# Summing the states of a scan on TensorE: identity matmul, or transposing matmuls with a copy and a turn back

## The chip, the cores and the metric

One core of a Trainium2 chip runs the whole program. The metric is the device time of one execution in microseconds (us). One execution was also recorded by the hardware profiler; stretches of it are given in us from the start of its span.

## The reference, cut to what matters

The network has an attention layer, six transformer layers, and a state-space layer with an adaptive norm around it. The change sits in the state-space layer. With 16 batch rows of 256 tokens, 256 inner channels d and 16 states n, it computes

```python
deltaA = jnp.exp(jnp.einsum('bld,dn->bldn', delta, A))
deltaB_u = (delta * h)[..., None] * Bm[:, :, None, :]

def step(state, t):
    dA_t, dBu_t, c_t = t
    state = dA_t * state + dBu_t
    y_t = jnp.einsum('bdn,bn->bd', state, c_t)
    return (state, y_t)
...
y = ys.transpose(1, 0, 2) + h * D_param
y = y * _silu(res)
return y @ out_proj_w
```

The einsum in `y_t` is the sum over the 16 states that the title speaks of.

## The kernel before, in words

Activations are kept with features on the partitions and tokens along the free dimension. The state-space stage (class `StateSpace`, run after the transformer) works on eight groups of two batch rows, so a tile is 128 channels by 512 tokens in f32. The 256 channels are two halves, k = 0 and 1, and one scan handles one state n of one half: 32 scans a group, numbered i = 2n + k.

For each i there are these steps: `DA` (ScalarE: the exponential, the decay), `DB` (the input, written to PSUM; for half of the first fourteen states and for the last two it is one VectorE product, kind "D", for the other seven it is four matmuls on TensorE, kind "E"), `SC` (VectorE: the scan itself), `HC` (GpSimd: the state times C) and `Y` (TensorE: adds `HC`'s tile to a sum in PSUM, by a matmul with the identity as the stationary operand; `start` on the first state, `stop` on the last). The two sums `y0` and `y1` have a PSUM bank each, `du` has two, and the other four banks are one pool, `bank()`, which serves `DB`, the transposes and every projection.

After the sums come `YK` (VectorE: y + D u, for each half), `GY` (GpSimd: times the gate), `PY` (TensorE: the output projection) and `XT` (VectorE: the residual). Then a second norm, one more matrix (`MY`, `ME`) and the output.

Before the scans of a group stand its own norm and projections: `L1` (four transposes), `ST`/`AG` (statistics), `RS` (GpSimd: the power -1/2), `NB`, `XN` (ScalarE: normalise, four instructions), `L2` (four transposes back), `HT`, the convolution `PX`, `U`, `PD`, `XD`, `PZ`, then `EE`, `WW`, `LL`, `W2`, `ZF` (the softplus and what follows from it), `DU`, `TD` (transposes for the "E" states), their copies `DT`, and `CDU` (ScalarE: a copy to PSUM for the "D" states). `DG` (ScalarE) scales the identity by B for the "E" states.

No scheduler decides the order: inside `manual_schedule` the instructions of each engine stand in the order in which the steps are called, and `SSM_ORDER` writes that order out. `YK0@2` means: in pass p, do `YK` of half 0 for group p - 2. So one pass mixes the ends of group p - 2, the scans of group p - 1 and the start of group p. A pass opens with `L1` of the new group, the last two `HC` and the last four `Y` of the old one, and `YK`; `DA05`, `DT0`, `DT1` and `DB05` of the next scans follow. In the profile, `Y` is L1434, `YK` L1440, `HC` L1428, `SC` L1424, `DB` L1415 and L1418, `DA` L1409, `DT` L1380, `CDU` L1384, `XN` L1226, `PY` L1450, `XT` L1458; `L1`, `L2` and `M3` share L1204.

Of the kernel before, what the change touches and what calls it, by code (L numbers as in the profile page):

```python
# [10 lines left out]
F32 = mybir.dt.float32  # L11
# [6 lines left out]
P = 128  # L18
B, S, D = 16, 256, 128
NT = S // P  # L20
NTOK = B * S
G = 2
NG = B // G
GT = G * S
# [15 lines left out]
DI, NS, DTR, KC = 256, 16, 64, 4  # L40
# [513 lines left out]
class Transformer:  # L554
# [330 lines left out]
    def Y(self, g, b, i):  # L885
        if i == 0:
            g.py[b] = self.one.take([P, S], "py")
        for h in range(4 * i, 4 * i + 4):
            self.c.nc.tensor.matmul(  # L889
                g.py[b],  # L890
                g.l.wvo[:, h, :],
                self.at[:, h, :],
                start=(h == 0),
                stop=(h == HEADS - 1),
            )
# [136 lines left out]
    def group(self, n):  # L1032
        g = Ctx()
        g.layer, g.b0 = n // NG, n % NG * G
        g.l = self.layers[g.layer]
        g.q = {(k, b, t): Ctx() for k in range(2) for b in range(G) for t in range(NT)}
        for name in ("ss", "r", "qT", "x2", "s", "mx", "pp", "sm", "pT", "pa", "py", "fp"):
            setattr(g, name, {})
        return g
# [47 lines left out]


SSM_ORDER = """
L1@0 HC30@2 ST@0 AG@0 HC31@2 Y28@2 Y29@2 Y30@2 RS@0 YK0@2 Y31@2 YK1@2 DA05@1 GY0@2 BT00@1 NB@0 DT0@1  # L1090
DT1@1 DA03@1 DB05@1 GY1@2 DA01@1 BT03@1 CDU@1 DA00@1 MY@3 DB01@1 XN@0 SC05@1 ME@3 L2@0 SC01@1 PY@2
DA04@1 HC01@1 DB02@1 SC02@1 DB04@1 MA@3 HC02@1 XT@2 SC04@1 HT@0 DB00@1 DA06@1 PX0@0 HC05@1 DA07@1
DG06@1 DA09@1 DA08@1 M3@3 SC00@1 DB07@1 SC07@1 Y01@1 HC00@1 U0@0 Y00@1 DB03@1 MO@3 DB08@1 SC03@1
# [17 lines left out]
class StateSpace:  # L1111
# [318 lines left out]
    def Y(self, g, i):  # L1430
        n, k = divmod(i, NC2)
        if n == 0:
            g.y[k] = self.dp.tile([P, GT], F32, tag=f"y{k}", name=f"y{k}")
        self.c.nc.tensor.matmul(g.y[k], self.c.ident, g.hc[i], start=(n == 0), stop=(n == NS - 1))  # L1434

# [63 lines left out]
    def group(self, i):  # L1501
        g = Ctx()
        g.i, g.b0 = i, i * G
        g.x = self.c.xT[:, i * GT : (i + 1) * GT]
        g.u = g.rs = g.z = g.e = None
        for name in ("px", "pr", "pz", "td", "dT", "bt", "cn", "dg", "da", "db", "s", "hc", "y", "yk"):
            setattr(g, name, {})
        return g

# [269 lines left out]
```

## Time and profile before

| | |
|---|---|
| time, median of 3 runs | 3700.16 us (3696.62 to 3700.87) |
| time of the profiled execution | 3697.34 us, its span 3695.6 us |
| busy over the span | PE 97%, DVE 90%, ACT 77%, POOL 71% |
| first and last scan of the state-space stage | about 3187 to 3672 us |
| `Y`, L1434 | 512 matmul records (two for each of 256 steps), 244.8 us busy |
| `SC`, L1424 | 256 scans, 301.1 us busy, 1208 ns each |

PE is TensorE, PEld its weight loads, DVE is VectorE, ACT is ScalarE, POOL is GpSimd. A wait row names the waiting engine and line, who ended the wait, and the total in us, the number and the longest. A timeline row has the start, the length, the engine, the line, and output <- inputs; a bracket at its end is the idle time just before it and what ended that.

### The profile page before, as it was taken

The page shows a single profiled execution, that of the slowest core. Times are in us where ns is not written, and L with a number is a line of the kernel's source. Part 1 is how long each engine was busy: PE and PEld are TensorE (multiplying, and loading weights), DVE is VectorE, ACT ScalarE, POOL GpSimd, SP SyncE. Part 2 cuts the span into 40 slices and gives each one's busy share as a digit, 9 for nine tenths or more (in the row PEclk, how much of TensorE's full clock was granted, in tenths as well). Part 3 has the DMA queues.
Part 4 walks back from the last instruction along what each step waited for, and adds up shares of the span by engine and source line. Part 5 has one row for each costly group of instructions (what it writes and reads, how often), then busy time and mean ns, then how long its engine had stood idle before and what let it go on. Part 6 is the DMA issues. An engine that isn't in the chain of part 4 may idle for free.

```text
span 3695.6 us, 104087 instructions
## 1 busy us (share of the span) xinstructions
PE 3581.4 (97%) x44976; PEld 2183.2 (59%) x44976; DVE 3343.1 (90%) x4735; ACT 2830.4 (77%) x4056; POOL 2616.4 (71%) x1668
## 2 busy tenths in 40 slices
PE   9999599999999999999999999999999999899997
PEld 5555366666666666666666666666666566555554
DVE  5675599999999999999999999999999998699997
ACT  3676477877877878778778777787788787889895
POOL 2231577777787777877877877777778886588887
PEclk7999699999999999999999999999999999999999
DMA  1100001000010000100001000000000000344442
GB/s 29 38 8 2 1 7 37 5 7 6 6 37 6 6 7 4 37 6 6 7 6 36 7 6 6 13 28 7 6 6 16 12 6 15 99 110 113 112 113 74
DMA packets 85672, 97.15 MB, mean 26 GB/s; under 512 B 9417, under 2 KB 56669, under 8 KB 84445
## 3 DMA queue, kind: packets, MB, share of 16 engines
q1 hardware_dynamic: 85212, 90.49, 9.0%
q8 instruction: 353, 5.78, 0.7%
q14 instruction: 107, 0.87, 0.1%
HBM read 75.26 MB, written 3.94 MB: 21 GB/s over the span
## 4 chain that ended last, share of the span: by engine, by line
PE 75%; ACT 5%; DVE 4%; issue 3%; POOL 1%; DVEq 0%; POOLq 0%; ACTq 0%
PE banks L889 18%; PE banks L679 16%; PE banks L868 10%; PE banks L965 7%; PE banks L810 6%; PE banks L753 4%; PE y L1434 4%; PE banks L1010 3%; ACT kT L770 2%; PE db L1418 2%; DVE s L1424 2%; PE px L1275 1%; ACT qT L770 1%; PE banks L780 1%; POOL u L741 1%
## 5 line engine op out<-in xcount | busy, mean ns | idle before, releaser
L726 POOL TENSOR_TENSOR u<-u,w 128x1024 f32<-128x1024 f32 x384 | 901.8, 2365 | 232.1 <-DVE w L707 149.0
L741 POOL TENSOR_TENSOR u<-u,r 128x1024 f32<-128x1024 f32 x384 | 720.5, 1903 | 129.5 <-DVE r L737 129.5
L679 PE MATMUL banks<-wqk,F 128*128 128x512 f32 x1536 | 727.3, 607 | 3.4 <-DVE w L707 3.4
L889 PE MATMUL banks<-at,wvo 128*128 128x256 f32 x3072 | 711.7, 382 | 0.1
L889 PEld LDWEIGHTS banks<-at,wvo 128*128 128x128 f32 x3072 | 571.7, 190 | 121.5 <-issue 44.6
L689 ACT ACTIVATE sq<-banks 128x512 f32<-128x512 f32 x768 | 425.9, 595 | 239.7 <-DVE u L695 226.1
L707 DVE TENSOR_TENSOR w<-banks,sinl 128x512 f32<-128x512 f32 x768 | 498.4, 673 | 33.0 <-PE banks L679 23.5
L695 DVE TENSOR_TENSOR u<-banks,cosl 128x1024 f32<-128x1024 f32 x384 | 463.7, 1208 | 10.6 <-PE banks L679 9.2
L679 PEld LDWEIGHTS banks<-wqk,F 128*128 128x128 f32 x1536 | 274.9, 191 | 314.4 <-issue 270.0
L719 DVE TENSOR_REDUCE ss<-sq 128x16 f32<-128x1024 f32 x384 | 454.3, 1194 | 3.5 <-ACT sq L689 0.6
L879 ACT COPY at<-banks 128x1024 f32<-128x1024 f32 x384 | 365.8, 1021 | 105.8 <-PE banks L868 105.7
L849 POOL TENSOR_TENSOR pp<-pp,sm 128x1024 f32<-128x1024 f32 x192 | 366.0, 1914 | 62.6 <-ACT sq L689 27.9
L868 PE MATMUL banks<-pT,xw 32*128 32x512 f32 x3072 | 388.6, 613 | 5.2 <-DVE w L707 2.4
L810 PEld LDWEIGHTS banks<-kT,qT 64*32 64x32 f32 x24576 | 262.5, 105 | 151.5 <-ACT sq L689 72.2
L1424 DVE TENSOR_TENSOR_SCAN s<-da,db 128x512 f32<-128x512 f32 x256 | 301.1, 1208 | 18.8 <-PE db L1418 5.6
L810 PE MATMUL banks<-kT,qT 64*32 64x64 f32 x24576 | 295.6, 225 | 3.9 <-issue 3.8
L770 ACT COPY qT<-banks 128x1024 f32<-128x1024 f32 x192 | 194.1, 1014 | 120.3 <-PE banks L753 120.3
L965 PE MATMUL banks<-hT,w 128*128 128x512 f32 (+1 forms) x576 | 265.8, 598 | 4.7
L823 DVE TENSOR_REDUCE mx<-banks 128x16 f32<-128x1024 f32 x192 | 233.1, 1214 | 37.4 <-PE banks L810 29.5
L1434 PE MATMUL y<-hc,ident 128*128 128x512 f32 x512 | 244.8, 604 | 18.9 <-POOL hc L1428 17.2
L868 PEld LDWEIGHTS banks<-pT,xw 32*128 32x128 f32 x3072 | 164.2, 186 | 155.0 <-issue 122.3
L753 PE MATMUL banks<-ident,u 64*128 64x64 f32 x6144 | 228.5, 227 | 24.1 <-POOL u L741 24.1
(235 smaller groups left out, 6210.6 us busy)
## 6 DMA issues: line engine op xcount, KB each, us to landing
btd<-bc SPq DMA_DIRECT2D x72, 512.0 KB
bte<-bc SPq DMA_DIRECT2D x56, 256.0 KB
xw<-xw SPq DMA_DIRECT2D x96, 96.0 KB
wqk<-in_Wqk SPq DMA_DIRECT2D x6, 1024.0 KB
wv<-in_LWvT SPq DMA_DIRECT2D x6, 512.0 KB
wo<-in_Wo SPq DMA_DIRECT2D x6, 512.0 KB
xin<-in_x SPq DMA_DIRECT2D x8, 256.0 KB
out<-ot SPq DMA_DIRECT2D x8, 256.0 KB
```

The source lines that it names most:

```text
L679: nc.tensor.matmul(q.p[:, x], self.F[:, g.b0 + b, o : o + P], g.l.wqk[:, k, x, :], start=True, stop=True)
L689: self.c.nc.scalar.activation(q.sq[:, x], q.p[:, x], AF.Square)
L695: self.c.nc.vector.tensor_tensor(q.u.rearrange("p h x d -> p x h d"), q.p, g.l.cosl[:, t, k].unsqueeze(2).to_broadcast([P, 2, HEADS, DH // ...
L707: self.c.nc.vector.tensor_tensor(q.w[:, :, x], q.p[:, 1 - x], g.l.sinl[:, t, k, x, :].unsqueeze(1).to_broadcast([P, HEADS, DH // 2]), ALU. ...
L719: self.c.nc.vector.tensor_reduce(g.ss[b][:, t, k, :], q.sq.rearrange("p x h d -> p h x d"), AX.XY, ALU.add)
L726: self.c.nc.gpsimd.tensor_tensor(q.u, q.u, q.w, ALU.add)
L741: self.c.nc.gpsimd.tensor_tensor(uf, uf, g.r[b][:, t, k, :].unsqueeze(2).to_broadcast([P, HEADS, DH]), ALU.mult)
L810: nc.tensor.matmul(s[qs, e, j, :], qT[es, j, qs], kT[es, j, ks : ks + 2 * W], start=False, stop=True, skip_group_check=True,)
L868: self.c.nc.tensor.matmul(g.pa[b, t, w // 2][:, w % 2, :], self.xw[b][qs, t, k, :], g.pT[b, t][qs, k, :], start=(k == 0), stop=(k == 1),)
L889: self.c.nc.tensor.matmul(g.py[b], g.l.wvo[:, h, :], self.at[:, h, :], start=(h == 0), stop=(h == HEADS - 1),)
L965: self.c.nc.tensor.matmul(p[0:n, x, :], g.l.w1[:, w : w + n], g.hT, start=True, stop=True)
L1434: self.c.nc.tensor.matmul(g.y[k], self.c.ident, g.hc[i], start=(n == 0), stop=(n == NS - 1))
```

## The change

`Y` no longer multiplies by the identity from the left with 512 columns at once. It takes the `HC` tile in four blocks of 128 columns, each the stationary operand of a transposing matmul against the identity, and adds these to the bank, so that the bank holds the sum with tokens on the partitions. Two new steps follow for each half: `YC` (ScalarE) copies the bank to SBUF, and `YB` (TensorE) turns the four blocks back into a bank of the four-bank pool, which `YK` then reads. In the order, `YC0` stands ahead of `Y31`, and `YB0`, `YC1`, `YK0`, `YB1`, `YK1` follow it.

```diff
-L1@0 HC30@2 ST@0 AG@0 HC31@2 Y28@2 Y29@2 Y30@2 RS@0 YK0@2 Y31@2 YK1@2 DA05@1 GY0@2 BT00@1 NB@0 DT0@1
+L1@0 HC30@2 ST@0 AG@0 HC31@2 Y28@2 Y29@2 Y30@2 RS@0 YC0@2 Y31@2 YB0@2 YC1@2 YK0@2 YB1@2 YK1@2 DA05@1 GY0@2 BT00@1 NB@0 DT0@1
 DT1@1 DA03@1 DB05@1 GY1@2 DA01@1 BT03@1 CDU@1 DA00@1 MY@3 DB01@1 XN@0 SC05@1 ME@3 L2@0 SC01@1 PY@2
 ...
     def Y(self, g, i):
         n, k = divmod(i, NC2)
         if n == 0:
-            g.y[k] = self.dp.tile([P, GT], F32, tag=f"y{k}", name=f"y{k}")
-        self.c.nc.tensor.matmul(g.y[k], self.c.ident, g.hc[i], start=(n == 0), stop=(n == NS - 1))
+            g.yt[k] = self.dp.tile([P, G * NT, P], F32, tag=f"y{k}", name=f"y{k}")
+        for j in range(G * NT):
+            self.c.nc.tensor.matmul(
+                g.yt[k][:, j, :],
+                g.hc[i][:, j * P : (j + 1) * P],
+                self.c.ident,
+                is_transpose=True,
+                start=(n == 0 and j == 0),
+                stop=(n == NS - 1),
+                skip_group_check=True,
+            )
+
+    def YC(self, g, k):
+        g.ys[k] = self.tile([P, G * NT, P], f"ys{k}", 1)
+        self.c.nc.scalar.copy(g.ys[k], g.yt[k])
+
+    def YB(self, g, k):
+        g.y[k] = self.bank([P, GT], "yb")
+        for j in range(G * NT):
+            self.c.nc.tensor.transpose(g.y[k][:, j * P : (j + 1) * P], g.ys[k][:, j, :], self.c.ident)
```

The second line of the order is unchanged and shown because the prediction follows it.

More of the change, by code (lines that the diff above doesn't have):

```diff
@@ L1505, in group @@
         g.u = g.rs = g.z = g.e = None
-        for name in ("px", "pr", "pz", "td", "dT", "bt", "cn", "dg", "da", "db", "s", "hc", "y", "yk"):
+        for name in ("px", "pr", "pz", "td", "dT", "bt", "cn", "dg", "da", "db", "s", "hc", "y", "yt", "ys", "yk"):
             setattr(g, name, {})
```

## The prediction

> **What bounds the stage now.** I read the page first, then the stage cut into passes (from one YK0 to the next), then VectorE's waits within one pass, and last the timeline where two passes meet. The change touches only the state-space stage, some 485 of the 3695.6 us.
>
> From the page:
>
> ```profile
> PE 3581.4 (97%) x44976; PEld 2183.2 (59%) x44976; DVE 3343.1 (90%) x4735; ACT 2830.4 (77%) x4056; POOL 2616.4 (71%) x1668
> ...
> L1434 PE MATMUL y<-hc,ident 128*128 128x512 f32 x512 | 244.8, 604 | 18.9 <-POOL hc L1428 17.2
> ```
>
> The busy times of a full pass and of the last one (length; busy of PE, PEld, DVE, ACT, POOL; granted clock, DMA):
>
> ```profile
> 3372.20:3433.54 61.34, 59.80 (x242) 33.68 (x242) 58.28 (x79) 55.60 (x100) 52.08 (x40) 1.00 0.39 113
> ...
> 3617.72:3675.30 57.58, 48.85 (x201) 28.06 (x202) 53.21 (x67) 30.93 (x58) 45.53 (x38) 1.00 0.27 69
> ```
>
> TensorE is busy 59.80 of 61.34 us, but VectorE 58.28: an engine that is freed cannot shorten the pass by more than the other one idles. All of VectorE's waits in that pass:
>
> ```profile
> DVE s L1424 <- PE db L1418: 1.0, 1, 1.0
> DVE yk L1440 <- PE y L1434: 0.5, 1, 0.5
> DVE s L1424 <- ACT xn L1226: 0.4, 1, 0.4
> ```
>
> These are 1.9 us; the other 1.15 us of idle time are gaps of about 0.1 us between instructions, and stay. So no relief of TensorE takes more than 1.9 us from a pass. Where passes meet, ScalarE and VectorE read:
>
> ```profile
> 3429.58 0.71 ACT L1409 ACTIVATE da<-z,am 128x512 f32<-128x512 f32 x1
> ...
> 3430.41 1.08 ACT L1380 COPY dT<-td 128x512 f32<-128x512 f32 x2
> ...
> 3430.65 4.05 PE L1434 MATMUL y<-hc,ident 128*128 128x512 f32 x8
> ...
> 3433.55 0.72 ACT L1409 ACTIVATE da<-z,am 128x512 f32<-128x512 f32 x1
> ...
> 3434.74 0.75 DVE L1440 SCALAR_TENSOR_TENSOR yk<-u,sv,y 128x512 f32<-128x512 f32 x1 [0.47 <-PE y L1434]
> ...
> 3435.93 1.50 ACT L1226 ACTIVATE xn<-ln,nb,r 128x128 f32<-128x128 f32 x4 [1.66 <-DVE nb L1221]
> ...
> 3437.65 1.88 PE L1450 MATMUL py<-yk,wout 128*128 128x512 f32 x4
> ...
> 3440.44 0.85 DVE L1458 SCALAR_TENSOR_TENSOR xT<-py,m1mod,xT 128x256 f32<-128x256 f32 x2
> ...
> 3441.20 1.21 DVE L1424 TENSOR_TENSOR_SCAN s<-da,db 128x512 f32<-128x512 f32 x1
> ```
>
> What matters is that ScalarE is early there: DA05, DT0, DT1, DA03, DA01, CDU, DA00 are done from 3429.58 to 3434.27 without waiting for any Y, and then it idles 1.66 us for NB.
>
> **TensorE's part.** In the chain of waits six Y records take 2.58 us, so one Y (two records) is 0.86 us. Four transposes of the same block size and type (L1204, L1376) take 0.44 us there (their four weight loads take 0.42 us beside them). A Y becomes four of them: 32 x (0.86 - 0.44) = 13.4 us fewer in a pass, and YB adds 2 x 0.44, so TensorE falls from 59.8 to about 47 us of work and is out of the bound. Were an accumulating transpose as dear as the 0.16 us that one L1376 record keeps PE busy (10.3 us over 64), a Y would be 0.64 us and TensorE 54 us: still not the bound, so the choice is free and I take 0.44. This uncovers the 1.0 us wait for DB; the 0.5 us of YK is replaced below. GpSimd waits 2.22 and 0.84 us for buffers that Y frees, and then runs without a pause from 3405.93 to the end of HC31 at 3433.53; 3 us earlier it is stopped by the last scan (SC31 ends 3431.64) and ends HC31 at 3431.64 + 1.32 = 3432.96. Bounds for that end: 3432.96 to 3433.53; I take the first, since the waits that made the delay are for Y.
>
> **What is added where passes meet.** ScalarE works in its order, so YC0 and YC1 stand in front of DA05, and all that I listed as early now queues behind Y31. Step by step, with durations of the rows named: Y30 is long done and YC0 over by 3432.98 (0.58 us, the DT copy of the same shape is 0.54, the output copy L1495 0.577). Y31 starts at 3433.0, 0.66 us by L1204's four after a wait: 3433.66. YC1: 3433.70 to 3434.28. YB0 is done at about 3434.1, YK0 (0.74) at 3434.85. YB1 takes the bank that YK0 frees, so it starts only then: done 3435.5, YK1 3436.3, where it was over at 3435.49 before. That costs VectorE 0.8 us by itself, but it is not what ends last. ScalarE: the seven early steps, 4.5 us without gaps, 3434.28 to 3438.75; XN 1.5 us, 3440.2 (before: 3437.43). DB02 waits for the same moment, since its bank is the one that XN frees. L2 and PY follow XN as before, PY 0.22 us after its end: 3440.42, done 3442.3. XT reads PY: 3442.35. DB04 stands behind PY on TensorE, done 3443.2, and SC04 starts at 3443.24, where it was at 3441.20. So VectorE is 2.0 us later after each meeting (2.6 with the other end of HC31).
>
> The wait of 1.0 us for DB later in the pass goes, as TensorE is 4 us ahead by then. Net 2.0 - 1.0 = 1.0 us a pass. A second round says the same: ScalarE has no gap from DA05 to the end of WW (36.6 us without the 1.18 us of waits for TensorE), W2 starts on VectorE right behind WW at 3408.43 and VectorE has no wait from there to SC31 (23.2 us), and SC31 to the end of YC1 is 2.65 us: 62.5 us against 61.34. I take +1.1 us a pass (bounds 1.0 and 1.6), six meetings: +6.6.
>
> The seventh (3617.72) has no XN behind it: DB05 waits for DT1, which is 1.4 us later: +1.4. In the tail YC and YB stand in the last chain, YK1 moves from 3675.25 to 3676.55: +1.3. Against this, the first pass has VectorE waiting 0.78 and 3.85 us for small products that stand behind five Y in TensorE's order; four or five Y give 1.7 to 2.1 us, together -2.5. Sum: 6.6 + 1.4 + 1.3 - 2.5 = +6.8 us. YC's 9.3 us of ScalarE work (16 x 0.58) are not added again: they lie in the chain above, and elsewhere ScalarE has 5.7 us idle in a pass. No DMA moves in its queue.
>
> **The clock.** From the PR matmuls (3422.6) to DB05, 12 us in every pass, TensorE would hold only transposes, about 13 Y, two TD, L1 and the YB: 7.5 us of work in 12. Rows of length, PE busy, clock:
>
> ```profile
> 3639.20:3642.60 3.40, 1.17 (x3) 1.00 0.31 121
> ...
> 2873.80:2877.20 3.40, 1.02 (x41) 0.92 0.02 5
> 2877.20:2880.60 3.40, 3.40 (x16) 0.58 0.00 0
> ```
>
> A stretch with a third of matmul work kept the clock, a slightly emptier one lost it. No row shows a long stretch of transposes alone, so the price has two ends. Clock held: nothing. Clock at half from before Y31 until dense work returns: Y31 0.5 us more (L1204's four took 1.12 at clock 0.50 in the tail, 0.60 elsewhere); DB05, MY and DB01, 2.8 us, would at worst double (MY 2.08 us at clock 0.50, 1.02 at 1.00) and then SC01 holds SC04 back by 2.5 us in all. A gain is excluded: a slower clock shortens nothing. I take 1.3 us a meeting, in the middle, because the three matmuls are themselves the dense work that ends it: 7 x 1.3 = +9, sum +16. The Trainium skill ("TensorE: Matmul & The Clock Gate", Part 4: PE-mode transpose) says that the full clock does not engage for transposing matmuls, since they do not count as busy in the same way. By that rule the sum would be +16, by the held row +6.8. Without the rule I would call the two about even, as the emptier row is so near to the stretch after the change; I lean to the dip.
>
> **To the runs.** +16 on the profiled 3697.34 is 3713.3, on the median 3700.16, which lies 2.8 higher, 3716; I say 3714. Some 0.2% (7.4 us) is what a measurement of this kernel can tell from no change.
>
> **The rivals.**
> 1. Copies cost as worked out, clock held: +6.8, range 0 to +12, 3699 to 3712. For it: 43% and 34% busy stretches at full clock in the last pass. Against: those were ordinary matmuls.
> 2. Faster: TensorE is the bound that the chain of waits suggests (Y alone is 27% of it in one pass), and the meeting costs less than the 1.0 us it gives back. It decides once SC04 comes less than 1.0 us later than now, which needs XN to end by 3439.2 (SC04 follows it by 3.0 us above), 4.9 us after YC1 instead of 5.9. At best 7 x 1.9 + 2.5 = -16: 3684; I would expect -8. Against it: ScalarE's order is fixed and its rows hardly vary.
> 3. The transposes do not get cheaper when they accumulate, or the clock stays at half for most of the pass: TensorE then needs 47 us stretched well over 61 and bounds again, +25 to +60, 3725 to 3760. Against: a dense TensorE regains its clock, as at 2880.60.
>
> **How the numbers follow.** Forecast (chain and dip, +8 to +25) 0.43, rival 1 0.33, rival 2 0.14, rival 3 0.10. The range must hold 0.8: from 3697, which takes in rival 1 and the weak end of rival 2, to 3730, which leaves out most of rival 3. Slower by over 0.2%: the forecast nearly whole, 0.41, under half of rival 1, 0.14, and rival 3, 0.10: 0.65. Faster: 0.11. Between: 0.24.
>
> **What would show it.** Right: a pass of 62.4 to 64 us with VectorE busy 58.3; PE busy near 47; the wait of SC for DB gone; XT or DB02 waiting for PY or XN, 2 to 4 us a pass; ScalarE idle before YC0 instead of before XN; POOL no longer waiting for Y. The dip shows as a clock below 1.00 in the 12 us before a meeting, and in a DB05 well over 1.05 us. Wrong: a pass of 60.5 us or less, or XN ending within 1 us of its old place after SC31 (5.8 us after it).

## The result, and the profile after

The changed kernel took 3719.81 us (median of 4 runs, 3711.29 to 3720.96), against 3700.2 before on the same chip: a ratio of 1.005, 95% interval 1.0033 to 1.0067. Slower, by 19.6 us, about 6 us more than forecast and inside the range. Its profiled execution took 3720.96 us, of which 3719.1 are the span; before, 3697.34 and 3695.6. The two profiles differ by 23.5 us, a little more than the medians, and the reading below accounts for these 23.5.

From the page of the kernel after, engine totals:

```profile
PE 3532.5 (95%) x45552; PEld 2230.1 (60%) x45552; DVE 3342.4 (90%) x4735; ACT 2840.6 (76%) x4072; POOL 2618.9 (70%) x1668
```

TensorE's busy time fell by 49 us over the run, VectorE's did not move, and the time went up. By passes (from one YK0 to the next; same columns as in the prediction), two passes of after:

```profile
3251.46:3315.50 64.04, 51.42 (x308) 37.29 (x308) 58.10 (x79) 55.43 (x99) 51.01 (x39) 0.97 0.37 105
...
3444.90:3509.49 64.59, 53.43 (x314) 38.74 (x314) 58.19 (x79) 57.19 (x103) 52.17 (x40) 0.96 0.40 110
```

TensorE does 51 to 53 us instead of 59.80 in a pass, VectorE the same 58.1, and the pass is 64 to 65 us instead of 61.34. The YK0 of the six passes from the first to the last start 64.04, 64.10, 65.33, 64.56, 65.24 and 63.60 us apart: 386.87 us against 367.80 before.

VectorE's waits in one pass of after, without the YK0 that begins it:

```profile
DVE s L1424 <- PE db L1418: 1.3, 2, 0.8
DVE yk L1458 <- PE yb L1452: 0.8, 1, 0.8
DVE s L1424 <- ACT da L1409: 0.7, 1, 0.7
DVE xT L1476 <- PE py L1468: 0.2, 1, 0.2
```

With the 1.10 us in front of YK0 that is 4.1 us, where the pass before had 1.9. All but one lie in the meeting of two passes. The timeline of after at one where the clock stood at 1.00 (the last scan of the older pass, SC31, ends at 3441.83):

```profile
3443.27 0.59 ACT L1447 COPY ys<-y 128x512 f32<-128x512 f32 x1 [2.60 <-PE y L1435]
...
3443.79 0.66 PE L1435 MATMUL y<-ident,hc 128*128 128x128 f32 x4 [0.56 <-POOL hc L1428]
...
3444.49 0.59 ACT L1447 COPY ys<-y 128x512 f32<-128x512 f32 x1 [0.63 <-PE y L1435]
3444.93 0.75 DVE L1458 SCALAR_TENSOR_TENSOR yk<-u,sv,yb 128x512 f32<-128x512 f32 x1 [1.09 <-PE yb L1452]
3444.97 0.72 ACT L1409 ACTIVATE da<-z,am 128x512 f32<-128x512 f32 x1
3445.59 1.06 ACT L1380 COPY dT<-td 128x512 f32<-128x512 f32 x2
...
3446.71 1.16 PE L1418 MATMUL db<-dg,dT 128*128 128x128 f32 x8 [0.26 <-ACT dT L1380]
...
3447.97 1.22 DVE L1424 TENSOR_TENSOR_SCAN s<-da,db 128x512 f32<-128x512 f32 x1 [0.67 <-ACT da L1409]
...
3449.34 1.50 ACT L1226 ACTIVATE xn<-ln,nb,r 128x128 f32<-128x128 f32 x4
3449.73 1.22 DVE L1424 TENSOR_TENSOR_SCAN s<-da,db 128x512 f32<-128x512 f32 x1 [0.53 <-PE db L1418]
...
3454.05 1.22 DVE L1424 TENSOR_TENSOR_SCAN s<-da,db 128x512 f32<-128x512 f32 x1
```

ScalarE idles 2.60 and 0.63 us in front of its two copies, and DA05, the DT, the other DA and CDU begin at 3444.97 only. The first scan's row names a DA, but DB05 (3446.71), which that scan also needs, ends only 0.1 us before it. XN ends at 3450.84, 9.0 us after SC31 (before: 5.8); the last line, SC04, starts 12.2 us after SC31's end (before: 9.56).

### The profile page after: what moved, and what is told of

Same layout as the page of the kernel before. It is cut to its first block, busy times and chain, and to the rows that moved or that the text cites. A ratio compares the mean times of both kernels' runs of the same rounds, so it can differ in the third digit from the quotient of the medians.

```text
span 3719.1 us, 105326 instructions
## 1 busy us (share of the span) xinstructions
PE 3532.5 (95%) x45552; PEld 2230.1 (60%) x45552; DVE 3342.4 (90%) x4735; ACT 2840.6 (76%) x4072; POOL 2618.9 (70%) x1668
## 4 chain that ended last, share of the span: by engine, by line
PE 70%; ACT 8%; DVE 5%; issue 4%; POOL 2%; POOLq 0%; DVEq 0%; ACTq 0%
PE banks L889 18%; PE banks L679 16%; PE banks L868 10%; PE banks L965 7%; PE banks L810 6%; PE banks L753 4%; PE banks L1010 3%; DVE s L1424 3%; ACT kT L770 2%; ACT da L1409 1%; PE db L1418 1%; ACT qT L770 1%; DVE db L1415 1%; PE banks L780 1%; POOL hc L1428 1%
## 5 line engine op out<-in xcount | busy, mean ns | idle before, releaser
L695 DVE TENSOR_TENSOR u<-banks,cosl 128x1024 f32<-128x1024 f32 x384 | 463.8, 1208 | 10.7 <-PE banks L679 9.1
L753 PEld LDWEIGHTS banks<-ident,u 64*128 64x128 f32 x6144 | 208.5, 141 | 73.1 <-issue 45.6
```

Of the source, the lines that this page charges most:

```text
L695: self.c.nc.vector.tensor_tensor(q.u.rearrange("p h x d -> p x h d"), q.p, g.l.cosl[:, t, k].unsqueeze(2).to_broadcast([P, 2, HEADS, DH // ...
L753: self.c.nc.tensor.matmul(q.pt[:, r, j, :], uf[rs, j * P : (j + 1) * P], self.c.ident[rs, rs], is_transpose=True, start=(j == 0), stop=Tru ...
```

## The experiments

Two theories stand from the prediction. The first: the loss is made by the copies and by what waits on them where passes meet. The second: it is made by TensorE's clock, which the transposes let fall. In the texts on record for the first four runs they are A and B. Later the first is split in two: what stands behind the copies on ScalarE (queue), or what reads their result (latency).

In one table: ratio to the kernel before with its 95% interval, the pass (YK0 to YK0) as it ranges over the six, and TensorE's clock.

| kernel | median us | ratio | pass, us | clock in the passes |
|---|---|---|---|---|
| before | 3700.2 | 1 | 60.9 to 61.5 | 1.00 |
| after | 3719.81 | 1.0050 (1.0033 to 1.0067) | 63.6 to 65.3 | dips, 0.95 mean |
| 1 no turn back | 3693.47 | 1.0001 (0.9992 to 1.0010) | 61.0 to 62.9 | dips |
| 2 copies, old sum | 3723.37 | 1.0084 (1.0068 to 1.0099) | 64.6 to 66.6 | mostly 1.00 |
| 3 half of the old sum | 3695.06 | 0.9997 (0.9987 to 1.0007) | 60.5 to 62.9 | dips |
| 4 ordinary blocks | 3727.79 | 1.0091 (1.0076 to 1.0106) | 65.1 to 65.6 | 1.00 |
| 5 copies unread | 3728.28 | 1.0078 (1.0066 to 1.0091) | 65.0 to 66.1 | dips |
| 6 copies late | 3699.21 | 1.0004 (0.9995 to 1.0013) | 60.6 to 62.0 | mostly 1.00 |
| 7 same order, old sum | 3700.94 | 1.0007 (0.9998 to 1.0016) | 61.2 to 61.9 | 1.00 |
| 8 copies early again | 3741.92 | 1.0121 (1.0107 to 1.0136) | 67.0 to 69.7 | dips, 0.90 mean |
| 9 copies and XT late | 3695.84 | 0.9999 (0.9990 to 1.0008) | 59.1 to 61.7 | dips |
| 10 the same, old sum | 3697.83 | 1.0006 (0.9997 to 1.0015) | 60.8 to 62.0 | 1.00 |
| 11 ordinary late | 3716.40 | 1.0060 (1.0047 to 1.0073) | 64.1 to 65.9 | 1.00 at meetings |
| 12 ordinary early | 3724.30 | 1.0076 (1.0064 to 1.0088) | 64.6 to 65.1 | 1.00 |

The medians of before beside runs 1 to 4, 5 to 7, 8 to 10 and 11 to 12 were 3695.34, 3696.86, 3695.09 and 3697.09; the ratios are to these.

**1. The transposing sum alone.** After, without YC and YB; YK reads the transposing bank as it lies, and the turn back is left out.

```diff
-... YC0@2 Y31@2 YB0@2 YC1@2 YK0@2 YB1@2 YK1@2 DA05@1 ...
+... YK0@2 Y31@2 YK1@2 DA05@1 ...
-            g.yk[k], g.u[:, k, :], self.sv[:, 2, k : k + 1], g.y[k], ...
+            g.yk[k], g.u[:, k, :], self.sv[:, 2, k : k + 1], g.yt[k].rearrange("p j t -> p (j t)"), ...
```

> The changed kernel without YC and YB: YK reads the transposing bank as it is, so the turn back is left out of the computation. Theory A (the loss is the queue: YC stands ahead of ScalarE's early steps, and YB ahead of YK): the meeting of two passes is as before the change, the waits for DB and for Y go, and a pass is about 60 us against 61.3: 3685 to 3691. Theory B (the loss is the clock that transposing matmuls let drop): the clock dips remain, some 1.3 us a meeting, and eat that gain: 3694 to 3706. Rival C (transposes do not relieve TensorE, PE busy stays near 60 us a pass): no gain and no dip, 3697.

3693.47 us, ratio 1.0001: the whole loss is gone with the copies and the turn back, and TensorE's 10 us a pass bring nothing. The time lies between the ranges of A and B: the meetings are as before, as A said, but A's gain did not come, and there are dips, as B said. Rival C is out, as TensorE does get its 10 us. Two passes (window query, columns as above), one with the clock up and one with dips:

```profile
3372.42:3433.46 61.04, 49.28 (x306) 35.84 (x306) 58.70 (x81) 55.67 (x100) 52.09 (x40) 1.00 0.40 114
3555.94:3618.21 62.27, 52.34 (x302) 38.72 (x302) 56.97 (x71) 56.21 (x100) 51.58 (x40) 0.92 0.40 109
```

The first is 0.3 us shorter than a pass before, the second, in which the clock dips, 1.0 longer than the same pass before (61.30). Why so little comes of the relief is seen at the one wait inside a pass that the prediction gave away, in the timeline of this run:

```profile
3400.72 1.16 PE L1418 MATMUL db<-dg,dT 128*128 128x128 f32 x8 [1.50 <-DVE s L1424]
...
3401.29 0.72 ACT L1409 ACTIVATE da<-z,am 128x512 f32<-128x512 f32 x1
...
3402.01 2.33 DVE L1424 TENSOR_TENSOR_SCAN s<-da,db 128x512 f32<-128x512 f32 x2 [0.75 <-ACT da L1409]
```

TensorE now idles 1.50 us, until VectorE's own scan releases it for this DB; and the scan waits 0.75 us for a DA of ScalarE, where it waited 0.99 for the DB. Relief of TensorE moves this wait to ScalarE and takes 0.24 us from it.

**2. The copies alone.** Before, with YC added and YK reading the copies; the sum is the old one.

```diff
-... YK0@2 Y31@2 YK1@2 DA05@1 ...
+... YC0@2 Y31@2 YC1@2 YK0@2 YK1@2 DA05@1 ...
```

> The kernel before with YC alone, at the places of the change: Y stays the identity matmul, ScalarE copies the sums to SBUF, YK reads the copies. Theory A: ScalarE's early steps start after Y31 here too, XN ends some 2.7 us later, XT waits for PY; no relief of TensorE pays for it: +2 to +2.6 us for each of six meetings, 3710 to 3716, clock 1.00 throughout. Theory B: no transposing matmul, no dip, the copy costs nothing that ends last: 3697 to 3702.

3723.37 us: two copies a pass, 0.6 us each, make a pass 3.8 us longer with no transpose in it. One such pass, with the clock at 1.00:

```profile
3377.52:3442.66 65.14, 61.04 (x244) 33.78 (x242) 59.17 (x79) 56.50 (x101) 52.22 (x41) 1.00 0.38 106
```

The kind was as expected from A, the size twice that. The waits of VectorE's scans in some five passes (3315 to 3630; us in total, times, longest), where before has 4.5 for DB and none for DA:

```profile
DVE s L1424 <- PE db L1418: 13.0, 10, 2.3
DVE s L1424 <- ACT da L1409: 5.5, 4, 1.4
```

Of the 3.8 us, 3.1 are lost at the meeting (12.66 us from the end of SC31 to SC04, before 9.58), and 0.7 in the rest of the pass (52.45 us, before 51.78).

**3. The same relief without transposing matmuls.** Before, with Y adding only the first 256 of 512 columns from the second state on (half of the sum is left out), so that TensorE saves about as much as with transposes.

```diff
-        self.c.nc.tensor.matmul(g.y[k], self.c.ident, g.hc[i], start=(n == 0), stop=(n == NS - 1))
+        w = GT if n == 0 else GT // 2
+        self.c.nc.tensor.matmul(g.y[k][:, 0:w], self.c.ident, g.hc[i][:, 0:w], ...)
```

> The kernel before, but after the first state Y adds only the first 256 of 512 columns (the rest of the sum is left out), by the ordinary identity matmul: 0.43 us a Y, as much as four transposes. It asks what the clock counts. If transposing matmuls count less than ordinary ones (theory B's ground), the clock stays 1.00 in the last 12 us of each pass and the time is 3685 to 3691. If only the share of busy time counts, the clock dips there as in the kernel without the turn back, and the times of the two are within 4 us of each other.

3695.06 us, ratio 0.9997, the same as run 1 within their intervals (the profiled execution, 3683.58 us, was the shortest of ten). And the clock falls here too, with ordinary matmuls; two stretches of this run:

```profile
3500.00:3510.00 10.00, 8.48 (x36) 5.07 (x34) 9.14 (x18) 9.95 (x18) 7.22 (x6) 1.00 0.12 41
3510.00:3520.00 10.00, 10.00 (x39) 6.56 (x39) 8.19 (x9) 7.88 (x12) 6.14 (x5) 0.66 0.60 185
```

So dips come with less work on TensorE, whether it transposes or not.

**4. The change without transposing matmuls.** After, with ordinary matmuls of the same four blocks against the identity, same layout.

```diff
-                is_transpose=True,
```

> The changed kernel with the four blocks of a Y as ordinary matmuls against the identity in place of transposing ones; YC and YB unchanged. TensorE then needs 0.86 us or more for a Y again, about 61 us a pass, and the clock should stay 1.00. Theory A: the meeting costs what it costs with transposes, and nothing is given back: TensorE and the meeting add, 3715 to 3740. Theory B: no dip, so at most a few us over the kernel before: 3697 to 3708.

3727.79 us, inside A's range and far outside B's. A pass of it:

```profile
3384.87:3450.47 65.60, 62.96 (x442) 51.96 (x442) 57.78 (x78) 56.48 (x102) 52.21 (x40) 1.00 0.38 105
```

The clock is 1.00 throughout, and the loss is larger than in after. (TensorE has even more to do here than before the change, 62.96 us against 59.80.) With runs 1 to 3 this makes a square, in us of a pass that no dip touched: old sum without copies 61.3, relief without copies 61.0 to 61.1, copies without relief 65.1 to 65.6, both (after, its sixth pass) 63.6. The copies cost, and the relief gives 1.5 to 2.0 us of it back, but only where they have made room for it.

**5. Copies that nobody reads.** Run 1 with the two copies put back at their places.

```diff
-... YK0@2 Y31@2 YK1@2 DA05@1 ...
+... YC0@2 Y31@2 YC1@2 YK0@2 YK1@2 DA05@1 ...
```

> After, with the two copies YC0 and YC1 of a pass kept at their places in ScalarE's order but read by nobody: YB is left out, YK reads the transposing bank as it lies (the turn back is left out, so the values per token are out of place). Queue theory: what costs is the place of the copies in ScalarE's order, ahead of DA05 to XN; that stays, so most of the cost stays: 3706 to 3716 us, XN still ending about 8 to 9 us after SC31. Latency theory: what costs is that YK, and PY and XT behind it, come later by copy and transposes; that is gone here, so 3692 to 3700 us, as with no copies at all.

3728.28 us: above the range of the queue theory, and far from that of the latency theory. The timeline of this run at a meeting (SC31 ends at 3445.47):

```profile
3446.89 0.58 ACT L1447 COPY ys<-y 128x512 f32<-128x512 f32 x1 [3.62 <-PE y L1435]
...
3448.11 0.58 ACT L1447 COPY ys<-y 128x512 f32<-128x512 f32 x1 [0.64 <-PE y L1435]
...
3450.32 2.08 PE L1418 MATMUL db<-dg,dT 128*128 128x128 f32 x8 [2.26 <-ACT dT L1380]
...
3452.51 1.22 DVE L1424 TENSOR_TENSOR_SCAN s<-da,db 128x512 f32<-128x512 f32 x1 [2.79 <-PE db L1418]
3452.95 1.51 ACT L1226 ACTIVATE xn<-ln,nb,r 128x128 f32<-128x128 f32 x4
```

The work that costs is not the sum's way back but the seven steps behind the copies: DT1 comes late, so DB05, so the first scan of the next states; the idle time that YK's two waits took in after stands here in one piece, 2.79 us, in front of that scan. XN ends 9.0 us after SC31, as in after. Not all of the 31 us is the queue itself: in four of the five meetings from 3317 to 3579, DB05 takes 2.04 to 2.08 us, as here, against 1.16 at a clock of 1.00, behind the 2.26 us for which TensorE waited for DT1.

**6 and 7. The copies later.** Run 6 is after with another order and nothing left out: the copies stand behind DA00 and ahead of XN, SC05 goes ahead of YK0, SC01 ahead of YK1, and PY and XT come later. Run 7 is the old sum in that order.

```diff
-L1@0 HC30@2 ST@0 AG@0 HC31@2 Y28@2 Y29@2 Y30@2 RS@0 YC0@2 Y31@2 YB0@2 YC1@2 YK0@2 YB1@2 YK1@2 DA05@1 GY0@2 BT00@1 NB@0 DT0@1
-DT1@1 DA03@1 DB05@1 GY1@2 DA01@1 BT03@1 CDU@1 DA00@1 MY@3 DB01@1 XN@0 SC05@1 ME@3 L2@0 SC01@1 PY@2
-DA04@1 HC01@1 DB02@1 SC02@1 DB04@1 MA@3 HC02@1 XT@2 SC04@1 HT@0 DB00@1 DA06@1 PX0@0 HC05@1 DA07@1
-DG06@1 DA09@1 DA08@1 M3@3 SC00@1 DB07@1 SC07@1 Y01@1 HC00@1 U0@0 Y00@1 DB03@1 MO@3 DB08@1 SC03@1
+L1@0 HC30@2 ST@0 AG@0 HC31@2 Y28@2 Y29@2 Y30@2 RS@0 Y31@2 DA05@1 BT00@1 DT0@1
+DT1@1 DA03@1 DB05@1 DA01@1 BT03@1 CDU@1 DA00@1 YC0@2 YC1@2 DB02@1 SC02@1 HC02@1 NB@0 XN@0 YB0@2 MY@3 SC05@1
+YK0@2 GY0@2 DB01@1 YB1@2 ME@3 L2@0 SC01@1 YK1@2 HC01@1 GY1@2 DA04@1 DB04@1 MA@3 SC04@1 HT@0 DB00@1 DA06@1 PX0@0
+HC05@1 PY@2 DA07@1
+DG06@1 DA09@1 DA08@1 M3@3 SC00@1 DB07@1 SC07@1 XT@2 Y01@1 HC00@1 U0@0 Y00@1 DB03@1 MO@3 DB08@1 SC03@1
```

> After, with another order at the meeting and nothing left out: YC0 and YC1 stand behind DA05, DT0, DT1, DA03, DA01, CDU and DA00 and ahead of XN in ScalarE's order, VectorE takes SC05 ahead of YK0 and SC01 ahead of YK1, PY and XT come later (XT after SC07). Theory that the copies cost by what they hold up: the loss of about 22 us in the stage goes, 3688 to 3702 us, passes of 60 to 62 us. Theory that the added work itself costs (16 copies, 64 transposes, a clock below 1.00): 3710 to 3722 us, passes still 63 to 65 us.

> Before's sum (ordinary matmuls, no copy, no transposes back) in the order of the run with the late copies. It tells how much of that run's time is the order's own. If the order by itself takes away waits of VectorE at the meeting: 3685 to 3695 us. If it only shifts them: 3695 to 3702 us. If XT and PY now come too late for the norm that reads them: over 3704 us, and then the run with late copies can't be read as the cost of the copies alone.

3699.21 and 3700.94 us, ratios 1.0004 and 1.0007: with all its copies and transposes the change costs nothing that can be measured, and the order by itself gains nothing. The timeline of run 6 at a meeting (SC31 ends at 3432.73):

```profile
3434.17 0.71 ACT L1410 ACTIVATE da<-z,am 128x512 f32<-128x512 f32 x1
...
3434.79 1.19 ACT L1448 COPY ys<-y 128x512 f32<-128x512 f32 x2
...
3436.77 1.51 ACT L1227 ACTIVATE xn<-ln,nb,r 128x128 f32<-128x128 f32 x4 [0.78 <-DVE nb L1222]
```

And a whole pass of it, columns as above:

```profile
3376.47:3437.78 61.31, 50.12 (x315) 36.58 (x314) 57.82 (x79) 56.76 (x102) 52.15 (x41) 1.00 0.43 113
```

Both copies now run back to back without a wait, in the time in which ScalarE idled before XN; XN ends 5.55 us after SC31.

**8. The copies back, and only they.** Run 6 with YC0 and YC1 moved to their old places on ScalarE, all else as in run 6.

```diff
-L1@0 HC30@2 ST@0 AG@0 HC31@2 Y28@2 Y29@2 Y30@2 RS@0 Y31@2 DA05@1 BT00@1 DT0@1
-DT1@1 DA03@1 DB05@1 DA01@1 BT03@1 CDU@1 DA00@1 YC0@2 YC1@2 DB02@1 SC02@1 HC02@1 NB@0 XN@0 YB0@2 MY@3 SC05@1
+L1@0 HC30@2 ST@0 AG@0 HC31@2 Y28@2 Y29@2 Y30@2 RS@0 YC0@2 Y31@2 YC1@2 DA05@1 BT00@1 DT0@1
+DT1@1 DA03@1 DB05@1 DA01@1 BT03@1 CDU@1 DA00@1 DB02@1 SC02@1 HC02@1 NB@0 XN@0 YB0@2 MY@3 SC05@1
```

> The run with the late copies, changed in one thing: YC0 and YC1 stand again where the changed kernel has them in ScalarE's order, ahead of DA05, DT0, DT1, DA03, DA01, CDU and DA00, while YB, YK, PY and XT keep their late places, so that nobody is in a hurry for the copies. Queue theory: the copies cost by what stands behind them on ScalarE, so the loss comes back, 3712 to 3728 us, passes of 63.5 to 65.5 us, VectorE waiting for DA and DB at the meeting by 3 to 5 us more a pass. Latency theory (the late YK and XT of the mended order are what helped): 3695 to 3703 us.

3741.92 us, 43 more than run 6 for moving two instructions on one engine, and beyond what I expected. The waits of VectorE in some five passes of this run (3315 to 3630; us in total, times, longest):

```profile
DVE db L1416 <- ACT du L1385: 25.0, 5, 5.0
DVE s L1425 <- PE db L1419: 12.5, 11, 2.1
```

In this order VectorE reaches the product with CDU's result with nothing in between that could fill the time, so it stands still for 5.0 us a pass; the clock, 0.90 in the mean, has a part in the waits for DB. Run 8 differs from run 6 in nothing but the place of the copies, so in this order their place is the cause. In the changed kernel's own order runs 2 and 5 show the same loss, without transposes and without a reader, by other waits of VectorE.

**9 and 10. XT one scan later.** In runs 6 and 7 VectorE waited up to 1.6 us a pass for PY at XT (7.5 and 7.7 us in five passes). Both with XT behind SC03 in place of SC07.

```diff
-DG06@1 DA09@1 DA08@1 M3@3 SC00@1 DB07@1 SC07@1 XT@2 Y01@1 HC00@1 U0@0 Y00@1 DB03@1 MO@3 DB08@1 SC03@1
+DG06@1 DA09@1 DA08@1 M3@3 SC00@1 DB07@1 SC07@1 Y01@1 HC00@1 U0@0 Y00@1 DB03@1 MO@3 DB08@1 SC03@1 XT@2
```

> The run with the late copies, with XT one scan later (behind SC03 instead of SC07), nothing left out. In that run VectorE waited 1.5 us a pass for PY at XT, and the norm that reads XT began some 6 us later. If this wait is time on VectorE's path: 1.5 us less in each of seven passes, 3688 to 3693 us, faster than both kernels. If another wait takes its place: 3696 to 3702 us.

> Before's sum in the same order with the late XT, the partner of the run before it. Same two outcomes for XT: 3689 to 3694 us or 3697 to 3703 us. The difference between the two is what the relief of TensorE (about 13 us of a pass) is worth with the copies out of the way: nothing if VectorE bounds the pass, 1 to 1.5 us a pass (7 to 10 us in all) by the prediction's waits for DB and Y.

3695.84 and 3697.83 us, the first just under the upper range: another wait took the place (DB03 waits for U0, 6.1 and 8.3 us in five passes), and the ratios came down by 0.0005 and 0.0001, well within their intervals. The pair says again what the relief is worth with the copies out of the way: 0.9999 against 1.0006, intervals that overlap. None of these orders beats the kernel before by what can be measured; run 9 beats the changed kernel by 0.5%.

**11 and 12. The clock at the meeting.** After, with the last ten Y of a pass (11) or the first 22 (12) as ordinary matmuls of the same blocks.

```diff
-                is_transpose=True,
+                is_transpose=(n < NS - 5),     # 11;  12: (n >= NS - 5)
```

> After, with the last ten Y of a pass (Y22 to Y31) as ordinary matmuls of the same four blocks against the identity, the first 22 as transposing ones; same values, same layout, copies and turn back kept. TensorE gets some 4 us more work in the 20 us before each meeting and should hold its clock there. Clock theory (1.3 us of each meeting in the changed kernel is a lowered clock): 3708 to 3714 us with 1.00 in the 10-us windows around the meetings. Load theory (what matters there is how soon Y31 and then DB05 get through TensorE, and ordinary blocks are slower at that): 3720 to 3730 us, clock 1.00 or not.

> The counterpart: the first 22 Y of a pass as ordinary matmuls, the last ten as transposing ones. Clock theory: the emptier stretch before each meeting is as in the changed kernel, so the clock still falls there, and the time is as with transposes throughout, 3717 to 3723 us. Load theory: the same time too, 3715 to 3723 us, since Y31 and the DB05 behind it are as quick; but if the 9 us a pass that TensorE gets back in the first two thirds were worth anything to VectorE, 3724 to 3730 us.

3716.40 and 3724.30 us. Run 11 falls between its two ranges. Three stretches of it, the last two around a meeting (YK0 at 3439.30), the first in the middle of a pass where it still transposes:

```profile
3400.00:3410.00 10.00, 8.50 (x28) 4.18 (x27) 9.00 (x11) 8.20 (x15) 4.71 (x4) 0.76 0.27 53
3430.00:3440.00 10.00, 9.13 (x78) 8.51 (x76) 8.24 (x18) 5.24 (x16) 8.62 (x8) 1.00 0.71 183
3440.00:3450.00 10.00, 9.25 (x49) 6.34 (x50) 7.61 (x11) 10.00 (x23) 7.09 (x6) 1.00 0.18 61
```

Its meetings keep the clock, but YK0 waits 1.59 us there instead of 1.09, since ten ordinary Y take longer, and the dips that remain lie in the middle. The sum is the same as in after (ratios 1.006 and 1.005, overlapping intervals). From the end of SC31 to SC04 each of the six meetings takes 12.6 to 12.7 us (12.1 to 12.2 in after where the clock held), and the two passes with a dip in the middle are 1.5 and 1.9 us longer there than the second and the sixth. So the two dips at meetings that after has are traded for slower meetings and two dips elsewhere, and the sum shows nothing.

Run 12 keeps 1.00 in all six passes, with transposes in the last third of each; that the clock would still fall there was wrong. A pass of it:

```profile
3380.79:3445.87 65.08, 59.44 (x402) 47.13 (x402) 57.76 (x78) 56.53 (x102) 52.18 (x40) 1.00 0.38 106
```

Its meetings take 12.1 to 12.2 us, as in after without a dip, but from SC04 to the next SC31 a pass takes 52.9 us where after takes 51.4. So TensorE's relief in the first two thirds of a pass is worth some 1.5 us while the copies hold up ScalarE, as in run 4.

## Why the prediction was right, and where its working was not

**What bounds a pass: right, and more so than I put it.** I held that a freed TensorE could take at most 1.9 us from a pass. It takes 0.3 (run 1, 61.04 against 61.34), as VectorE's remaining wait passes to ScalarE, and L1221, the product of NB with GpSimd's result, takes 1.09 us on average in two passes where it took 0.86. Dips in some passes take that back.

**The meeting: right mechanism, the larger of my two ends.** I worked out SC04 as 2.0 us later if HC31 ends 1.32 us after SC31, and 2.6 if it ends as late as before. Measured: 12.2 - 9.56 = 2.66 us. HC31 ended at 3443.74, 1.91 us after SC31, as in before: GpSimd runs six HC without a pause from 3436.29 to that end, and its delay is its own work, not only its waits for Y, which fell from 17.9 us to 7.6 in five passes. This was the first mis-sized term: 0.6 us a meeting. XN's end I put 8.6 us after SC31; it was 9.0. XT, at the end of that chain, starts 11.3 us after SC31, as the chain with the later HC31 has it (10.7 + 0.6). But it waits only 0.26 us for PY, where I had VectorE wait 2 to 4 us at XT or DB02: by then VectorE had lost 3.1 us at YK0, YK1 and the first two scans (1.09, 0.81, 0.67, 0.53; 0.9 in all before), where I had 0.8 for YK1 alone. Two paths end within 0.3 us of each other, and run 5, in which YK reads neither a copy nor a turned-back sum, shows that the meeting is no shorter without the one through YK (12.1 us at the first, 13.6 to 14.8 at the others, with dips).

**What is given back: this step failed.** I took 1.0 us a pass off because the wait of a scan for DB in the middle of the pass would go. It did not. The timeline of after, in the middle of a pass:

```profile
3345.15 1.16 PE L1418 MATMUL db<-dg,dT 128*128 128x128 f32 x8 [1.50 <-DVE s L1424]
...
3345.74 0.72 ACT L1409 ACTIVATE da<-z,am 128x512 f32<-128x512 f32 x1
...
3346.45 2.33 DVE L1424 TENSOR_TENSOR_SCAN s<-da,db 128x512 f32<-128x512 f32 x2 [0.76 <-PE db L1418]
```

TensorE is idle for 1.50 us in front of this DB: it was never only TensorE's load that made it late, as the DB waits for VectorE's own scan before, and ScalarE's DA ends at the same moment. 0.99 us became 0.76. To see what is given back, count each pass from the end of SC31 in place of YK0, as a meeting, up to the start of SC04, and a rest. Before, the first meeting takes 9.0 us and the others 9.56 to 9.58, the rests 51.8 to 52.0. In after the four meetings that no dip touched take 12.1 to 12.2 and the rests 51.4 to 51.9. So such a meeting costs 2.64 us (the first 3.1), and a rest gives back 0.4 us at most, not 1.0. The second and the sixth pass are 2.2 us longer each, where I had +1.1.

**The clock: dips came, as leaned to, but fewer and dearer.** At 1.3 us in each of seven meetings I had +9. A mean clock of 0.96 or 0.97 need not cost anything: with it the rests of the second, fourth and sixth pass are still shorter than before. The price lies at the meetings at 3379.60 and 3509.49, where the clock falls on the meeting itself (0.74 in 3380 to 3390 us, 0.76 in 3510 to 3520 us). At the second (timeline of after, VectorE's lines):

```profile
3509.49 0.75 DVE L1458 SCALAR_TENSOR_TENSOR yk<-u,sv,yb 128x512 f32<-128x512 f32 x1 [1.70 <-PE yb L1452]
...
3511.50 0.75 DVE L1458 SCALAR_TENSOR_TENSOR yk<-u,sv,yb 128x512 f32<-128x512 f32 x1 [1.27 <-PE yb L1452]
...
3513.28 1.22 DVE L1424 TENSOR_TENSOR_SCAN s<-da,db 128x512 f32<-128x512 f32 x1 [0.95 <-PE db L1418]
...
3515.95 1.22 DVE L1424 TENSOR_TENSOR_SCAN s<-da,db 128x512 f32<-128x512 f32 x1 [1.45 <-PE ln L1204]
...
3520.26 1.22 DVE L1424 TENSOR_TENSOR_SCAN s<-da,db 128x512 f32<-128x512 f32 x1
```

These waits and the 0.29 of XT are 5.7 us, against 3.4 where the clock is 1.00 (DB05, the first of the two DB there, takes 1.92 us instead of 1.16). The last line, SC04, starts 14.5 us after the end of SC31 (3505.77), where it was 12.2: 2.3 us for each of the two dips, 4.5 together. From SC31 to SC31 the six passes are 386.84 - 367.83 = 19.0 us longer: 16.3 for the meetings at a held clock, 4.5 for two dips where I had 7.8 for six, less 1.8 given back in the rests.

**The ends of the stage.** I had -2.5 us for the first pass: VectorE's waits for the small products fell from 3.85 to 2.12 and from 0.78 to 0.68 us as meant, but another, for the first of these products, rose from 3.35 to 4.28, and two scans now wait 0.93 us for DB: the first SC31 ends 0.35 us later, not 2.5 earlier. From the last SC31 to the end of the span it is 83.9 us against 79.75: +4.1, with the clock at 0.84 from 3638.33 to 3698.52; I had 1.4 + 1.3 and one dip of 1.3, which is 4.0.

So 0.35 + 19.0 + 4.1 makes the 23.5 us. The forecast of +16 came near in part by luck, because errors of size stood against each other: the six meetings, less what was given back, were worth 14.5 us, not 6.6, the first pass 0.35, not -2.5, and the dips in the six meetings 4.5, not 7.8. Of the signs that I had named, VectorE's busy time, ScalarE's idle time before YC0 and the dips came; the loss of the wait for DB and the 47 us of TensorE did not, five of the six passes lie above my 62.4 to 64 us, and GpSimd still waits for Y. The rival with the clock held (+6.8) was wrong by its meetings; the faster one asked for XN less than 4.9 us behind YC1 and got 5.8; in the slow one a Y gets no cheaper or the clock stays low for most of a pass, and a Y did get cheaper (0.57 us in run 6, against 0.86), and the lowest mean clock of one of the six is 0.93.

**TensorE's work** I put at 47 us a pass; it is 50.1 at a clock of 1.00 (run 6). A Y of four transposes takes 0.57 us (90.7 us for 160 of them in run 6), not 0.44: they come one Y at a time, as HC delivers them, and four after a wait take 0.65. Nothing hung on it.

**The rule that I leaned on.** Run 3 has no transposing Y at all and falls to 0.66 in a stretch; run 12, with transposing Y in the last third of each pass, and run 6's pass above, with all Y transposing and TensorE at 50.12 of 61.31 us, hold 1.00. So transposing by itself does not bring the dips. TensorE has 58 to 63 us of work a pass in runs 4, 7, 10 and 12, which have none, and 49 to 53 in runs 1, 3, 6 and 9, which have some; which gap brings one stays open, as run 6 holds 1.00 from 3410 to 3420 us with TensorE busy for 5.69 of 10. The Trainium skill ("TensorE: Matmul & The Clock Gate", Part 4: PE-mode transpose) has the full clock not engage for transposing matmuls; these runs do not show that. The stretch of transposes alone that I found no row for stands in run 12: from 3434.6 to 3447.4 us, and at the same place in four more passes, TensorE has nothing else to do, is busy for 8.8 of 12.8 us, and the clock reads 1.00. In after the same stretch also reads 1.00 before the meeting at 3444.93, and ahead of the one at 3509.49 it falls, to 0.86 (3505.6 to 3509.0 us) and 0.50 (3509.0 to 3512.4). How a longer stretch behaves, or one that begins at a low clock, is not shown here. Its page "PSUM — Partial Sum Buffer" (Engine vs sequencer instructions) says that the queues of ScalarE, VectorE and GpSimd are strictly first in, first out; runs 6 and 8 show the price of that here, 43 us between two places of the same two copies.

## What to carry to other kernels

An instruction that waits for the last result of one stage costs what stands behind it on its engine, not its own 0.6 us: before adding one to a fixed order, list the steps behind it that were early, and put it behind them, where that engine idles anyway. Relief of the busiest engine is worth only what the next engine waits for it, and each such wait has to be followed to its other inputs: a wait named after TensorE may end no sooner because ScalarE or a buffer is due at the same time. When the sum over passes comes out right, look at the terms too.

## What the runs showed that I had not expected

TensorE's clock fell with less work on it also for ordinary matmuls, and where a dip falls decides what it costs: two passes of run 3 with a mean clock of 0.97 and 0.95 took 61.05 and 62.89 us. Where the copies stand first, ordering the rest well makes it worse: VectorE's work that filled the gap in after was gone in run 8, and its passes take 67.0 to 69.7 us instead of 63.6 to 65.3.
